# Side work inside a scan tile: its place on VectorE, its distance, PE's sums one tile later, and denser jobs in a four-layer scan network

## The chip, the cores and the metric

The kernel runs on one core of one Trainium2 chip. The metric is device time in microseconds from the first to the last instruction of one execution, with what little lies around it; the number given is the median of the runs. The engines are PE (matrix products), VectorE (DVE), ScalarE (ACT), GpSimd (POOL) and SyncE (SP, which here issues every DMA). Each works through a queue of its own in order.

## The reference

Four images of 64 x 64 positions (L = 4096) with 96 channels go through four layers. Each layer is a mixer and a feed-forward network, both with a residual. Layer 0's mixer is a gated recurrence, those of layers 1 to 3 are selective scans. Cut to what matters, with the convolution, the orders and the feed-forward lines shortened:

```python
def _L0_conv_ref(x, ...):            # gated recurrence, 96 x 16 states
    ...
    def step(h, ins):
        A_t, B_t, C_t, d_t, u_t, g_t = ins
        d = d_t[..., None]
        h_new = d * (A_t * h) + d * (B_t * u_t[..., None])
        y = g_t * jnp.sum(C_t * h_new, axis=-1)
        return (h_new, y)
...
def _L1_conv_ref(x, ...):            # layers 2 and 3 alike
    xz = jnp.einsum('bhwc,ec->bhwe', x, in_proj_w)
    xp, z = jnp.split(xz, 2, axis=-1)
    xc = silu(depthwise_conv_3x3(xp) + conv_b)
    xs2 = jnp.stack([x_hw, x_wh], axis=1)
    xs = jnp.concatenate([xs2, jnp.flip(xs2, axis=-1)], axis=1)
    dts, Bmat, Cmat = jnp.split(x_dbl, [DT_RANK, DT_RANK + D_STATE], axis=2)
    delta = jax.nn.softplus(dts + dt_projs_bias[None, :, :, None])
    ...
    def step(h, inp):
        u_l, dl, b_l, c_l = inp
        dA = jnp.exp(dl[..., None] * A)
        h = dA * h + (dl * u_l)[..., None] * b_l[:, :, None, :]
        y = jnp.einsum('bkdn,bkn->bkd', h, c_l)
        return (h, y)
    ...
    y = _layernorm(y, out_norm_w, out_norm_b)
    y = y * jax.nn.silu(z)
    return jnp.einsum('bhwd,cd->bhwc', y, out_proj_w)
...
h = jax.nn.relu(_qlinear(x, W1, b1))   # feed-forward, products in 8-bit floats
y = _qlinear(h, W2, b2)
```

A selective scan runs over 192 channels with 16 states each, in four orders: by rows, by columns, and both backwards.

## The kernel before

**Stages.** `gated` (line 1039) does layer 0's recurrence for the four images in 384 tiles of 128 x 512. `scans` (line 855) does the selective scans of layers 1 to 3: 12 stages, one for each layer and image, of 384 tiles each. What lies between two recurrences of an image (the sum over orders, the norms, the output product, the feed-forward network, the input product, the 3 x 3 convolution) is a job, `between` (line 612), that is worked off in small steps beside the tiles of another image. Image 3's last job (line 1282) runs alone at the end.

**A scan tile.** A tile is one state n of one chunk of 128 rows (64 channels in each of two orders) over T = 1024 positions. The loop over k (line 986) issues for each tile, in this order: `carry(k-1)` (ScalarE copies the last column of h), `c_rows(k+2)` (SP loads the row of C, spread over the partitions), `decays(k+2)` (ScalarE's exp), `b_rows(k+1)` (PE spreads the row of B into PSUM, the tile bc), `scan(k)` (VectorE's product bc <- du, bc, then its scan h <- da, carry, bc), `times_c(k-1)` (GpSimd multiplies h by C in place), `store` of a finished chunk, the side work, and `accumulate(k-2)` (PE sums h into acc, a double bank in PSUM). There are two bc buffers, so b_rows(k+1) waits for scan k-1; four buffers of h, and one acc.

**Order.** `InOrder` (line 70) chains every instruction of an engine to the one issued before it, so the engines run exactly in the order in which the Python code issues. All instructions are recorded by its inner function, which is why the profile gives line 80 for each of them; they are told apart by the names of their tiles.

**Side work.** It consists of generators. `pump` (line 136) runs a generator up to its next `yield`; `yield True` means that the next piece needs one of two PSUM banks (`bank`, `release`), and a bank comes free at the end of the tile (`settle`). A tile pumps `chain` (prepares the next chunk: dt_proj, softplus; `prepare_chunk`, line 806) and `segment` (the next x_proj with its remainder on VectorE; `prepare_segment`, line 758) once each, and then calls `work`, which lets the job make steps. `Job.step` (line 711) adds `rate` to a credit, capped at 2.0, and pumps every chain of the job's round once per whole credit. A consumer that stands one `yield` behind its producer is therefore one step behind it, which can be in the same tile. A job has rounds: `first` (loads), then `feeds`, `mixers` and `joins` at once, then `second`, then `convolves` and `takes` at once. Norms collect in `pending` until `logarithms` (line 245) takes their Ln together; a strip waits for that. If a stage's job is unfinished 28 tiles before the stage's end, it is worked off there without tiles (lines 999 to 1003).

**The generators that change**: `Norm.measure` (line 227; `moments`, line 209, is VectorE's bn_stats and bn_aggr, tiles st and mv), `join_orders` (line 318; PE's y_t, tile yt), `mixer_out` (line 358; y_c, GpSimd's u times z, out_proj, VectorE's x1), `feed_forward` (line 428; ff_xt, VectorE's xq, ff_h, GpSimd's hq, ff_y, x2), `first` in `between`.

## Time and profile before

| | us |
|---|---|
| median of three runs (20,117.64 to 20,146.91) | 20,146.27 |
| profiled execution | 20,152.58 |
| its span | 20,150.8 |

| engine | busy us | share | instructions |
|---|---|---|---|
| PE | 16,417.6 | 81% | 70,656 |
| VectorE | 17,808.5 | 88% | 13,848 |
| ScalarE | 12,295.0 | 61% | 19,373 |
| GpSimd | 15,531.3 | 77% | 10,470 |

The largest groups are GpSimd's h <- h, c (4608 times 2.358 us), VectorE's scan (4608 times 2.347) and product (4608 times 1.210), and PE's sums into acc (36,864 passes). A busy share over the whole run mixes the gated stage, where VectorE is not the fullest engine, with the scans. PE's clock is granted by a throttle; over the run it is 0.817 of full speed, and a busy PE is not PE at its peak.

### The profile page before, as it was taken

To read this page: it belongs to the slowest core of one execution; us is meant where nothing else is said; L and a number is where in the kernel's file an instruction comes from. 1 tells how busy PE (TensorE), PEld (TensorE's weight loads), DVE (VectorE), ACT (ScalarE), POOL (GpSimd) and SP (SyncE) were. 2 spreads that over 40 slices of the span, in tenths; PEclk is the share of its full clock that TensorE was granted. 3 is DMA by queue.
4 is the path that set the end of the run, shared out by engine and by line. 5 is a ranking of instruction groups with operands and counts; after the bars stand their busy time and mean duration, and the time that the engine had idled before them with its cause. 6 is when DMAs were issued, how large, how long until landed. Compare 5 with 4: busy or idle time off the path is not lost. (4 is left out here: it accounts for less than half of the span.)

```text
span 20150.8 us, 220842 instructions
## 1 busy us (share of the span) xinstructions
PE 16417.6 (81%) x70656; PEld 4838.3 (24%) x70656; DVE 17808.5 (88%) x13848; ACT 12295.0 (61%) x19373; POOL 15531.3 (77%) x10470
## 2 busy tenths in 40 slices
PE   8998788787888787788788888788788888887776
PEld 3332121121122222222222222222222222222223
DVE  6665999999999998999999999989999999999881
ACT  4444665665665665665665666666666666666553
POOL 3434888888888887888888888878888888878882
PEclk9898796786887797897887887887887887888775
DMA  0002666666666666666666676666676666676661
GB/s 20 16 18 69 165 181 174 166 186 167 168 184 171 164 179 175 166 182 180 167 187 171 167 189 167 169 180 169 170 187 171 168 187 168 170 188 161 172 169 44
DMA packets 1234532, 3148.68 MB, mean 156 GB/s; under 512 B 428049, under 2 KB 428177, under 8 KB 1227217
## 3 DMA queue, kind: packets, MB, share of 16 engines
q1 hardware_dynamic: 1233360, 3134.55, 58.6%
q8 instruction: 554, 9.08, 0.2%
q14 instruction: 618, 5.05, 0.1%
HBM read 2819.18 MB, written 314.57 MB: 156 GB/s over the span
## 5 line engine op out<-in xcount | busy, mean ns | idle before, releaser
L80 POOL TENSOR_TENSOR h<-h,c 128x1024 f32<-128x1024 f32 x4608 | 10834.6, 2358 | 2827.5 <-ACT carry L80 1727.5
L80 DVE TENSOR_TENSOR_SCAN h<-da,carry,bc 128x1024 f32<-128x1024 f32 x4608 | 10814.5, 2347 | 608.7 <-POOL carry L80 10.3
L80 PE MATMUL acc<-h,stacked 64*64 64x512 f32 x36864 | 6179.1, 747 | 498.7 <-POOL h L80 493.8
L80 ACT ACTIVATE da<-delta,decay 128x1024 f32<-128x1024 f32 x4608 | 5280.9, 1147 | 1648.9 <-DVE h L80 1601.8
L80 DVE TENSOR_TENSOR bc<-du,bc 128x1024 f32<-128x1024 f32 x4608 | 5574.5, 1210 | 611.2 <-PE bc L80 586.0
L80 PE MATMUL bc<-bs,sel 96*128 96x512 bf16 x9216 | 3346.9, 451 | 2071.8 <-DVE h L80 2054.6
L80 ACT COPY carry<-h 128x1 f32<-128x1 f32 x3456 | 649.0, 188 | 3533.7 <-DVE h L80 3529.1
L80 PEld LDWEIGHTS <-sel 96*128 96x128 bf16 x9216 | 551.3, 101 | 6988.6 <-DVE h L80 5085.7
L80 PEld LDWEIGHTS acc<-h,stacked 64*64 64x64 f32 x36864 | 1132.5, 153 | 3286.5 <-issue 1699.7
L80 ACT ACT_TABLE_LOAD x1133 | 1453.6, 1283 | 41.6 <-DVE mv L80 22.5
L80 POOL TENSOR_TENSOR c<-h,c 128x512 f32<-128x512 f32 x384 | 485.7, 1265 | 970.5 <-ACT c L80 614.8
L80 PE MATMUL conv<-pad,tap_lo 128*128 128x512 f32 x1728 | 917.5, 630 | 0.0
L80 PE MATMUL dt_proj<-rows,w 12*128 12x512 f32 x1152 | 828.0, 805 | 0.0
L80 ACT ACTIVATE du<-e,ones 128x1024 f32<-128x1024 f32 x576 | 660.8, 1147 | 228.8 <-POOL delta L80 223.2
L80 PE MATMUL x_proj_b<-u,xp 128*108 128x512 f32 x1152 | 671.9, 699 | 94.3 <-DMA xp<-in_ssm 59.0
L80 ACT ACTIVATE c<-c,l_bias 128x512 f32<-128x512 f32 x384 | 263.5, 686 | 753.0 <-PE c L80 737.9
L80 POOL TENSOR_TENSOR delta<-delta,du 128x1024 f32<-128x1024 f32 x288 | 679.5, 2359 | 12.1 <-ACT du L80 12.1
L80 POOL TENSOR_TENSOR e<-e,du 128x1024 f32<-128x1024 f32 x288 | 679.4, 2359 | 2.4 <-ACT du L80 2.4
L80 POOL TENSOR_TENSOR du<-delta,u 128x1024 f32<-128x1024 f32 x288 | 679.4, 2359 | 0.7
L80 POOL TENSOR_TENSOR delta<-delta,e 128x1024 f32<-128x1024 f32 x288 | 678.5, 2356 | 0.1
L80 PE MATMUL x_proj_c<-u,xp 128*48 128x512 f32 x1152 | 624.3, 655 | 64.3 <-ACT rows L80 64.3
L80 PE MATMUL conv<-pad,tap_hi 128*128 128x512 f32 (+1 forms) x1152 | 638.5, 650 | 8.2 <-ACT u L80 8.2
(155 smaller groups left out, 16118.3 us busy)
## 6 DMA issues: line engine op xcount, KB each, us to landing
c<-cs SPq DMA_DIRECT2D x9216, 256.0 KB, 4.1
u<-u SPq DMA_DIRECT2D x288, 512.0 KB, 7.6
y<-y SPq DMA_DIRECT2D x1152, 128.0 KB, 2.4
y<-y SPq DMA_DIRECT2D x144, 512.0 KB, 5.6
xr<-x SPq DMA_DIRECT2D x224, 192.0 KB, 4.8
u<-u SPq DMA_DIRECT2D x288, 128.0 KB, 4.4
pad<-y SPq DMA_DIRECT2D x288, 128.0 KB, 4.6
z<-zl SPq DMA_DIRECT2D x96, 256.0 KB, 2.0
```

What stands on the lines that cost most here:

```text
L80: ins = f(*a, **k).ins
```

## The change

Within a tile the side work moves: `scan` takes it as a function, `beside`, and calls it between VectorE's product and its scan. `times_c` and `store` are issued ahead of the product. PE's sums come three tiles behind the scan instead of two, with five buffers of h instead of four. The carries of a new chunk are set to zero at tile 8 of the chunk before. `logarithms` at tile 11 comes behind that tile's carry and decays. The rates go from 1.4 to 1.65 (stage jobs), from 1.9 to 2.6 (the last layer's output jobs) and from 1.4 to 2.6 (layer 0's job), the cap of the credit from 2.0 to 3.0. Several `yield`s are added, and a norm's statistics are taken in three pieces. The halves of chunk 1 are swapped, so that all chunks have the row order first: C then has 32 rows instead of 48, and the selector of B 128 columns instead of 192. GpSimd adds the second bias in one instruction instead of four, and x2 shares xh's buffer.

```diff
-CHUNKS = (((0, 0), (64, 1)), ((0, 1), (64, 0)), ((128, 0), (128, 1)))
+CHUNKS = (((0, 0), (64, 1)), ((64, 0), (0, 1)), ((128, 0), (128, 1)))
...
-NC3 = 48
+NC2 = 2 * NS
...
         def measure(self, src, width, e):
-            mv = moments(src, width)
+            st = sb(5, "st", [128, G, 6])
+            mv = sb(5, "mv", [128, G, 2])
+            for g in range(G):
+                dve.bn_stats(st[:, g, :], src[:, g, 0:width])
+                if g % 2:
+                    yield
+            for g in range(G):
+                dve.bn_aggr(mv[:, g, :], st[:, g, :])
             yield
...
             yield pair == 0
+        yield
         norm = Norm()
...
         normalise(yt, yt, DI, norm.r, norm.nm)
+        yield
         yield True
...
                 pool.tensor_tensor(v[0:m], v[0:m], z[0:m], ALU.mult)
-                yield m == 64
+                yield
+        yield True
         ps = bank("out_proj")
...
             yield
+        yield
         x1 = sb(2, "x1", [128, G, C])
...
         normalise(xh, x1, C, norm.r, norm.nm)
+        yield
         yield True
         ps = bank("ff_xt")
         transpose_strip(ps, xh, 0, C)
+        yield
+        yield
         yield
...
         pool.tensor_copy(hq[:, 2, :], late, saturate=False)
+        yield
         yield True
         ps = bank("ff_y")
...
-        for g in range(G):
-            pool.tensor_tensor(y[:, g, :], y[:, g, :], b[:, 3 : 3 + C], ALU.add)
-        yield
-        x2 = sb(1, "x2", [128, G, C])
+        pool.tensor_tensor(y, y, b[:, None, 3 : 3 + C].to_broadcast([128, G, C]), ALU.add)
+        yield
+        x2 = sb(1, "xh", [128, G, C])
         pool.tensor_tensor(x2, x1, y, ALU.add)
+        yield
         yield
         sp.dma_start(out=tokens(dst, s), in_=x2)
         if layer < 3:
+            yield
             norm = hold["norm", s] = Norm()
...
                 load_y(im, 0, hold)
+            yield
             yield
             yield
...
-            self.credit = min(self.credit + self.rate, 2.0)
+            self.credit = min(self.credit + self.rate, 3.0)
...
+        def start(i):
+            if i.first:
+                carries[i.chunk] = sb(2, f"carry{i.chunk}", [128, NS])
+                pool.memset(carries[i.chunk], 0.0)
+            i.carry = carries[i.chunk]
...
-        def scan(k):
+        def scan(k, beside):
             i, n = tiles[k]
             da, b = live.pop((k, "da")), live.pop((k, "b"))
-            if n == 0 and i.first:
-                carries[i.chunk] = sb(2, f"carry{i.chunk}", [128, NS])
-                pool.memset(carries[i.chunk], 0.0)
-            i.carry = carries[i.chunk]
             dve.tensor_tensor(b, i.du, b, ALU.mult)
-            h = live[k, "h"] = sb(4, "h", [128, T])
+            beside()
+            h = live[k, "h"] = sb(5, "h", [128, T])
...
-                if n == 11:
-                    logarithms()
+                if n == 8 and nxt is not None:
+                    start(nxt)
...
-            if 0 <= k - 1 <= last:
-                carry(k - 1)
-            if k + 2 <= last:
-                c_rows(k + 2)
-                decays(k + 2)
-            if k + 1 <= last:
-                b_rows(k + 1)
-            if k <= last:
-                scan(k)
-            if 0 <= k - 1 <= last:
-                times_c(k - 1)
-            if k >= 3 and (k - 3) % NS == NS - 1:
-                store(items[(k - 3) // NS])
-            if k <= last:
+            def beside():
                 pump(chain)
                 pump(segment)
                 if n == 13:
@@
                     if item.chunk == 2:
                         drain(segment, work)
                 work()
-            if 0 <= k - 2 <= last:
-                accumulate(k - 2)
+
+            if 0 <= k - 1 <= last:
+                carry(k - 1)
+            if k + 2 <= last:
+                c_rows(k + 2)
+                decays(k + 2)
+            if n == 11:
+                logarithms()
+            if k + 1 <= last:
+                b_rows(k + 1)
+            if 0 <= k - 1 <= last:
+                times_c(k - 1)
+            if k >= 4 and (k - 4) % NS == NS - 1:
+                store(items[(k - 4) // NS])
+            if k <= last:
+                scan(k, beside)
+            if 0 <= k - 3 <= last:
+                accumulate(k - 3)
             settle()
...
-        gated(images, Job(between(images[0], 0), patience=1), pl0)
+        gated(images, Job(between(images[0], 0), 2.6, patience=1), pl0)
...
-            jobs[-1].append(Job(between(im, layer - 1), 1.4))
+            jobs[-1].append(Job(between(im, layer - 1), 1.65))
...
-            jobs[-1].append(Job(between(im, 3, im.dst), 1.9))
+            jobs[-1].append(Job(between(im, 3, im.dst), 2.6))
```

## The prediction

> **What bounds the kernel now.** First the page's part 1 and the windows by stage, to split the run; then the waits and the groups of VectorE between 1890 and 19640 us; then the timeline of single tiles. The run is a gated stage (33 to 1750 us), preparations (to 1890), 4608 scan tiles (to 19,679) and a tail (to 20,150.8). Windows (us; PE, PEld, DVE, ACT, POOL busy; clock):
>
> ```profile
> 1640.00:1742.00 102.00, 101.60 (x281) 41.41 (x280) 72.79 (x89) 45.65 (x101) 40.34 (x64) 1.00 0.07 18
> 1742.00:1800.00 58.00, 45.53 (x100) 17.06 (x98) 1.24 (x2) 24.97 (x49) 9.57 (x32) 0.85 0.14 34
> 1800.00:1842.00 42.00, 31.30 (x71) 12.70 (x70) 0.00 (x0) 10.66 (x17) 6.51 (x9) 0.88 0.35 82
> ...
> 1890.00:19640.00 17750.00, 14405.78 (x64735) 3970.86 (x64735) 16511.66 (x11807) 11242.20 (x17195) 14686.67 (x8955) 0.81 0.65 174
> ```
>
> See: PE is full at the end of the gated stage; then 100 us in which VectorE does nothing (the job beside layer 0 is not finished, and runs alone); in the scans VectorE is 93% busy. It is the bound there. One tile of it, then one with side work, from the timeline (start, duration):
>
> ```profile
> 1907.57 1.21 DVE L80 TENSOR_TENSOR bc<-du,bc 128x1024 f32<-128x1024 f32 x1
> 1908.91 2.35 DVE L80 TENSOR_TENSOR_SCAN h<-da,carry,bc 128x1024 f32<-128x1024 f32 x1
> 1911.17 0.71 DVE L80 BATCH_NORM_STATS2 st<-xr 128x6 f32<-128x96 f32 x4
> 1911.80 0.36 DVE L80 BATCH_NORM_AGGREGATE mv<-st 128x2 f32<-128x6 f32 x4
> 1912.08 1.20 DVE L80 TENSOR_TENSOR bc<-du,bc 128x1024 f32<-128x1024 f32 x1
> ```
>
> Product to scan: 1.34 us for a product of 1.21, so 0.13 us idle (the scan reads what the product writes). Scan to next: 2.26 for 2.35, so neighbours that don't depend on each other overlap by 0.09. A plain tile is 3.605 us (mean of the 3739 plain tiles when I list all starts). 4607 x 3.605 = 16,608; first scan to last is 17,787; the excess of 1179 us is 654 of waits and 524 of side work (577 tiles have some). Who VectorE and PE wait for there (us, times, longest):
>
> ```profile
> DVE bc L80 <- PE bc L80: 585.5, 350, 18.0
> DVE xq L80 <- PE ff_xt L80: 24.0, 27, 1.8
> DVE h L80 <- POOL carry L80: 10.3, 7, 1.6
> PE acc L80 <- POOL h L80: 493.1, 374, 5.3
> PE ff_xt L80 <- ACT xh L80: 191.9, 46, 6.1
> ```
>
> Behind each late bc I followed PE's queue back. Largest: out_proj behind GpSimd's u 80 us (34 tiles), ff_xt behind ScalarE's xh 74 (35), PE just busy 63 (63), y_t behind its DMA 59 (11), two layer changes behind xp 36, acc behind GpSimd's h only 44 (44); the rest is spread. An example:
>
> ```profile
> 7963.82 0.74 PE L80 MATMUL out_proj<-w,u 128*128 128x96 f32 x2 [4.51 <-POOL u L80]
> ...
> 7967.09 1.99 PE L80 MATMUL acc<-h,stacked 64*64 64x512 f32 x8
> ...
> 7969.01 0.72 PE L80 MATMUL bc<-bs,sel 96*128 96x512 bf16 x2
> ...
> 7969.77 1.23 DVE L80 TENSOR_TENSOR bc<-du,bc 128x1024 f32<-128x1024 f32 x1 [5.49 <-PE bc L80]
> ```
>
> Side work too close to its producer stops PE's queue, and the scan with it. Last the tail: 471 us after the last scan, with VectorE 21 of 200 us busy. Of image 2's eight last strips one is out before the last scan, the eighth at 19,845.6; image 3's job follows, with its column loads at 19,859.
>
> **The skill.** "VectorE: DVE Perf Modes", The DRAIN you can't avoid, has the next instruction start only when the pipe is empty, and a read after a write on the same engine need a semaphore; its section on two Vector instructions with no wait between them lets one that is not held start earlier. The trace bears out the second and third (0.13 us idle, against 0.09 overlap). "TensorE: Matmul & The Clock Gate", Part 1, says that PE's clock halves after idle windows: acc takes 1.09 or 1.98 us here. The same page calls VectorE's and ScalarE's queues strict FIFO: a waiting side instruction stops the tile's own.
>
> **The change, part by part** (against the profiled execution: 20,152.6 us, span 20,150.8; the median, 20,146.3, lies 6 us lower).
>
> 1. *Side work between product and scan.* Today a run of side instructions of length D costs D - 0.09 (the x_proj remainder: 0.66, measured excess 0.60). Between product and scan it overlaps at both ends and covers the 0.13 us: D - 0.30, a gain of 0.21 per tile. If a product does not let its successor overlap (the trace never shows that pair; product after product in the gated stage has a gap of 0.03), it is D - 0.19, a gain of 0.10. A norm's statistics are split over three steps, so more tiles get side work: counting yields under the kernel's rules (credit, two banks, logarithms) gives 576 tiles before (the trace has 577) and 883 after. D in all: 524 + 577 x 0.09 = 573, plus 26 of image 2's strips (part 4), plus some 25 for lost overlaps at the cuts: 624. New cost 624 - 883 x 0.30 = 360, gain 164; with 0.19, 456, gain 68. I take 140.
>
> 2. *Distance, rate 1.65, sums three tiles behind.* At 1.4 steps a tile, a consumer one step later falls into the same tile in 0.4/1.4 = 29% of cases. Two steps at 1.65 are never the same tile. out_proj and ff_xt get the second step: 154 us to some 30. ff_y likewise (18 to 8), y_t's first load a step of 2.2 us (59 to 40). Sums: PE's 493 us behind GpSimd go, but only 44 of them reached VectorE; to 5. Together -200. Against it: unchanged one-step pairs fall together more often (0.65/1.65 = 39%); convolutions get denser (a strip every 15.4 tiles for 18.3 by the count; a strip is some 17 us of PE at full clock: 30 convolution passes and 8 of in_proj and z at 0.43, which is what back-to-back passes take in the timeline, and the transposes; so +0.17 us per tile on a PE that is 88% busy there, 105.9 of 120 us at 14,497): +50. VectorE's side work now stands before the scan, 2.3 us earlier against ScalarE and PE; the added yields cover st, x1 and xq, but the remainder (190 times, one tile behind ScalarE) is uncovered: 0 to 40, taken 10. Last stage at 2.6: two steps can be one tile again (23%), and 24 strips for 17: waits 109 to some 150, +40. Sum -100. Bounds: -250 (all the gain, no cost) and +150 (convolutions at PE's limit, clock low).
>
> 3. *Carries ahead, logarithms after the decays, job finished earlier.* The 10 us behind carry go. At two layer changes the job's rest was worked off without scans just ahead of the next loads (SP busy 4.9 us with part_c); by the count the job ends 11 tiles ahead now: -20 of 36 + flush. GpSimd's four bias adds in one, fewer selector copies, 32 for 48 C rows: beside GpSimd's 17% idle, nothing. SP: x2's store is issued a step later, so blocks the c loads behind it less; nothing. Sum -30.
>
> 4. *Last stage at 2.6.* The same count for 1.9 puts image 2's first out strip at tile 369 (the trace: 370), the others after the scans. For 2.6 with the new yields all eight lie before tile 373 of 384, so the tail is image 3 alone. From the last scan: about 16 us to sums, store and landing, then as today from the column loads: 20,151 - 19,859 = 292. 308 for 471: -163. I take -160. If two strips slip out of the scans it is -120.
>
> 5. *Layer 0's job at 2.6.* The count finishes it at gated tile 330 of 384 (1.4: three of eight convolved, the trace agrees). The 92 us from 1750 to 1842 go. But PE's 77 us of it (45.5 + 31.3 above) move into a stage where PE is 99% busy once convolutions run; earlier windows leave some idle. Cost 60 to 84, taken 67: -25 (0 to -60).
>
> Sum: -140 - 100 - 30 - 160 - 25 = -455: 20,152.6 - 455 = 19,698, near 19,695 on the median's side.
>
> **Rivals.** (a) As summed: 19,695, own range 19,560 to 19,830; chance 0.52. (b) Distance only changes who waits: VectorE's side work waits itself for ScalarE and PE, and the product doesn't overlap. For: in-order queues, and the step rate rises with the yields. Against: two steps are a full tile. Leaves 160 + 25 + 30: 19,935; 0.23. (c) PE is never late except for its DMAs: waits 654 to 250, parts 1 and 5 at their best (164, 40), tail 160: -768, 19,380. For: PE never waits for GpSimd. Against: dense convolutions; 0.17. (d) Slower: PE becomes the bound in the dense stretches. At the low clock a tile's bc and acc are 1.04 + 1.98 us, with the shares of x_proj and dt_proj (0.4 at full clock) and of a convolution strip (17/15.4 = 1.1), doubled, 6 us; 11 x 108 convolution tiles and 384 of the last stage are 1570. From 0.3 us per such tile on (PE's mean over about 4 us) it eats 455; at 0.4 us: 20,320. Against: the clock is 0.87 to 0.94 in those windows, as PE is busy; 0.08.
>
> Chances: (a), (c) and most of (b) and a little of (d): faster 0.91, within 0.2% (about what this measurement can tell from no change) 0.03, slower 0.06. The range goes to (c) below and (b) above: 19,470 to 19,920.
>
> **What would show it.** Side work standing between product and scan with no idle ahead of the scan, tile excess D - 0.30. "PE acc behind POOL h" near zero; "DVE bc behind PE bc" near 400. No VectorE hole after the gated stage, last gated scan later by some 65 us. All of image 2's stores before the last scan, tail near 310. Wrong, if VectorE waits for ScalarE or PE in st, x, xq or rows by more than 100 us, or if PE's clock in the convolution windows falls.

## The result and the profile after

The changed kernel takes 20,024.88 us (median of five runs, 20,018.46 to 20,055.13); the kernel before, run on the same chip, takes 20,135.62. The ratio is 0.9949, 95% interval 0.9935 to 0.9964: faster by 0.5%, where 2.2% was forecast, and outside the forecast's range. The profiled execution has a span of 20,016.7 us, 134.1 less than that of before (the medians differ by 111: the profiled execution is the fastest of the five after, and the one before, at 20,152.58, lies above all five of before). (In the changed kernel the recording line is L78, for L80, and PE's sums read `twice` where they read `stacked`.)

The page, its first part and the groups of the scan:

```profile
PE 16405.8 (82%) x70656; PEld 4828.9 (24%) x70656; DVE 17721.0 (89%) x13832; ACT 12306.6 (61%) x19398; POOL 15475.3 (77%) x10086
...
L78 DVE TENSOR_TENSOR_SCAN h<-da,carry,bc 128x1024 f32<-128x1024 f32 x4608 | 10797.4, 2343 | 507.3 <-ACT norm L78 23.0
...
L78 PE MATMUL acc<-h,twice 64*64 64x512 f32 x36864 | 6198.0, 749 | 11.3 <-POOL h L78 10.8
...
L78 DVE TENSOR_TENSOR bc<-du,bc 128x1024 f32<-128x1024 f32 x4608 | 5571.2, 1209 | 656.2 <-PE bc L78 630.3
```

VectorE's instructions take what they took (the scan 2.343 us for 2.347, the product 1.209 for 1.210); the difference lies in its idle time and in where things stand. Splitting both traces in the same way, by the listing of all starts, gives the whole difference in four numbers (us):

| | before | after | difference |
|---|---|---|---|
| first scan tile starts (gated stage and preparation) | 1890.3 | 1958.9 | +68.6 |
| first to last scan: side work on VectorE | 524 | 338 | -186 |
| first to last scan: waits of VectorE | 654 | 817 | +163 |
| last scan to the end | 471.0 | 291.4 | -179.6 |

The middle two are what the 4607 steps from scan to scan take beyond 3.605 us each; 17,786.8 became 17,763.7 in all. Of the 186 us of side work, 159 stand in the tiles that have some and 27 in those that have none, which came out a little shorter (3.599 us for 3.605). So two parts of the change bring 366 us, and two others take 232 of them back.

Side work in its new place, read from the timeline of the changed kernel (the last column is the idle time of the engine before the instruction, and what ended it):

| start us | us | engine | instruction | waited before |
|---|---|---|---|---|
| 19629.05 | 1.21 | DVE | TENSOR_TENSOR bc<-du,bc x1 |  |
| 19630.17 | 0.54 | DVE | TENSOR_TENSOR x<-xr,out_proj x1 |  |
| 19630.74 | 0.74 | DVE | BATCH_NORM_STATS2 st<-x x4 |  |
| 19631.40 | 2.33 | DVE | TENSOR_TENSOR_SCAN h<-da,carry,bc x1 |  |
| 19633.65 | 1.21 | DVE | TENSOR_TENSOR bc<-du,bc x1 |  |
| 19634.76 | 0.37 | DVE | BATCH_NORM_AGGREGATE mv<-st x4 |  |
| 19635.05 | 2.32 | DVE | TENSOR_TENSOR_SCAN h<-da,carry,bc x1 |  |

The x starts 1.12 us after the product, which lasts 1.21: the product does let its successor overlap. The aggregate of 0.37 us makes its step 3.65 us, from 19631.40 to 19635.05, only some 0.05 more than a step without side work.

The groups above end in the idle time ahead of each group, and in who ended most of it: 630.3 us of the product's 656.2 lie behind PE's bc. The view of the waits, between 1958 and 19,680 us, has the other pairs (a selection of its rows):

| engine, tile | waits for | us | times | longest |
|---|---|---|---|---|
| DVE bc | PE bc | 630.3 | 335 | 21.3 |
| DVE rows | ACT bs | 42.2 | 21 | 4.0 |
| DVE st | DMA xr<-x | 30.9 | 16 | 3.1 |
| DVE x | PE out_proj | 25.2 | 21 | 3.4 |
| DVE st | ACT yt | 15.6 | 15 | 2.0 |
| PE acc | ACT y | 169.2 | 151 | 3.3 |
| PE in_xt | ACT xh | 132.8 | 41 | 8.6 |
| PE y_c | ACT yt | 80.1 | 29 | 5.0 |
| PE out_proj | POOL u | 79.3 | 40 | 5.4 |
| PE ff_xt | ACT xh | 47.8 | 36 | 4.1 |
| ACT xh | POOL norm | 348.4 | 136 | 7.2 |

PE's 493 us behind GpSimd's h are gone (7.9 are left), and ff_xt's 191.9 are 47.8. But VectorE's lateness behind PE, which was to fall to some 400, rose to 630, and a second kind stands beside it: VectorE itself waits in side work, 148 us in all for 41 before. Behind each late bc I followed PE's queue back again: out_proj 49 us (80 before), ff_xt 2 (74), acc 17 (44), y_t 78 (59); but in_xt behind ScalarE's xh 128 (3 before), y_c behind ScalarE's yt 65 (3), and PE just busy 124 (63). One in_xt, in the timeline:

| start us | us | engine | instruction | waited before |
|---|---|---|---|---|
| 7129.36 | 1.54 | ACT | ACTIVATE xh<-xr,norm x4 | 4.99 for POOL norm |
| 7129.88 | 1.52 | PE | MATMUL in_xt<-ident,xh x4 | 8.64 for ACT xh |
| 7131.33 | 1.99 | PE | MATMUL acc<-h,twice x8 |  |
| 7133.25 | 1.03 | PE | MATMUL bc<-bs,sel x2 |  |
| 7134.32 | 1.23 | DVE | TENSOR_TENSOR bc<-du,bc x1 | 6.54 for PE bc |

Read it upwards: VectorE is 6.54 us late for its row of B; the row stood in PE's queue behind the sums and those behind in_xt, which had waited 8.64 us for ScalarE, and ScalarE 4.99 us for GpSimd's norm. This is the pattern that the forecast showed for out_proj, one generator further on.

The stretches ahead of the scans, from the windows by stage:

| window us | length | PE busy | DVE busy | ACT busy | POOL busy | PE clock |
|---|---|---|---|---|---|---|
| 1477 to 1700 | 223 | 221.10 | 139.91 | 110.94 | 84.60 | 1.00 |
| 1700 to 1906 | 206 | 188.83 | 149.28 | 74.88 | 76.03 | 0.93 |
| 1906 to 1958 | 52 | 23.18 | 4.92 | 21.25 | 16.56 | 0.72 |

The hole of 100 us is gone, as forecast: the preparation takes 52 us, for 152. But the last gated scan comes at 1906.6 instead of 1738.0. The four images take 431.5, 482.6, 515.1 and 429.2 us, for 402.8, 438.6, 423.5 and 424.7. The first image has no job beside it at all, and is 29 us longer.

Last, the tail. All of image 2's stores are out before the last scan: the latest (out <- xh) is issued at 19,683.56, the last scan starts at 19,722.55. The page's row of VectorE's busy tenths in 40 slices, of some 500 us each, ends in a 4: in 291 of the last slice's 500 us the job of image 3 stands alone. In the kernel before the row ended in a 1, with 471 us of a slice of 504:

```profile
DVE  6656999999999999999999999999999999988884
```

### The profile page after: what moved, and what is told of

Same layout as the page of the kernel before. It is cut to its first block, busy times and chain, and to the rows that moved or that the text cites. A ratio compares the mean times of both kernels' runs of the same rounds, so it can differ in the third digit from the quotient of the medians.

```text
span 20016.7 us, 220305 instructions
## 1 busy us (share of the span) xinstructions
PE 16405.8 (82%) x70656; PEld 4828.9 (24%) x70656; DVE 17721.0 (89%) x13832; ACT 12306.6 (61%) x19398; POOL 15475.3 (77%) x10086
## 5 line engine op out<-in xcount | busy, mean ns | idle before, releaser
L78 POOL TENSOR_TENSOR h<-h,c 128x1024 f32<-128x1024 f32 x4608 | 10832.7, 2359 | 2723.7 <-ACT carry L78 1730.5
L78 DVE TENSOR_TENSOR_SCAN h<-da,carry,bc 128x1024 f32<-128x1024 f32 x4608 | 10797.4, 2343 | 507.3 <-ACT norm L78 23.0
L78 ACT ACTIVATE da<-delta,decay 128x1024 f32<-128x1024 f32 x4608 | 5280.9, 1148 | 1507.9 <-DVE h L78 1492.8
L78 PE MATMUL acc<-h,twice 64*64 64x512 f32 x36864 | 6198.0, 749 | 11.3 <-POOL h L78 10.8
L78 DVE TENSOR_TENSOR bc<-du,bc 128x1024 f32<-128x1024 f32 x4608 | 5571.2, 1209 | 656.2 <-PE bc L78 630.3
L78 PE MATMUL bc<-bs,sel 96*128 96x512 bf16 x9216 | 3388.1, 456 | 2351.0 <-DVE h L78 2338.8
L78 ACT COPY carry<-h 128x1 f32<-128x1 f32 x3456 | 648.7, 188 | 3203.7 <-DVE h L78 3198.8
L78 PEld LDWEIGHTS <-sel 96*128 96x128 bf16 x9216 | 551.1, 101 | 7287.9 <-DVE h L78 5440.5
L78 PEld LDWEIGHTS acc<-h,twice 64*64 64x64 f32 x36864 | 1130.6, 153 | 2798.4 <-issue 1924.1
L78 POOL TENSOR_TENSOR c<-h,c 128x512 f32<-128x512 f32 x384 | 485.5, 1264 | 1149.4 <-ACT c L78 783.5
L78 PE MATMUL conv<-pad,tap_lo 128*128 128x512 f32 x1728 | 927.1, 647 | 0.0
L78 ACT ACTIVATE du<-e,ones 128x1024 f32<-128x1024 f32 x576 | 661.2, 1148 | 352.3 <-POOL delta L78 347.5
L78 PE MATMUL dt_proj<-rows,w 12*128 12x512 f32 x1152 | 823.5, 801 | 6.8 <-ACT delta L78 6.8
L78 PE MATMUL x_proj_b<-u,xp 128*108 128x512 f32 x1152 | 707.5, 732 | 47.5 <-DMA xp<-in_ssm 12.6
L78 ACT ACTIVATE c<-c,l_bias 128x512 f32<-128x512 f32 x384 | 263.1, 685 | 772.6 <-PE c L78 771.2
L78 PE MATMUL x_proj_c<-u,xp 128*32 128x512 f32 x1152 | 625.0, 656 | 79.7 <-ACT rows L78 71.2
L78 POOL TENSOR_TENSOR delta<-delta,du 128x1024 f32<-128x1024 f32 x288 | 679.4, 2359 | 7.8 <-ACT du L78 7.8
L78 POOL TENSOR_TENSOR e<-e,du 128x1024 f32<-128x1024 f32 x288 | 679.3, 2359 | 2.4 <-ACT du L78 2.4
L78 POOL TENSOR_TENSOR du<-delta,u 128x1024 f32<-128x1024 f32 x288 | 680.3, 2362 | 0.1
L78 POOL TENSOR_TENSOR delta<-delta,e 128x1024 f32<-128x1024 f32 x288 | 678.5, 2356 | 0.1
L78 PE MATMUL conv<-pad,tap_hi 128*128 128x512 f32 (+1 forms) x1152 | 597.4, 620 | 3.5 <-ACT u L78 3.5
```

The source lines that it names most:

```text
L78: ins = f(*a, **k).ins
```

## The experiments

Fourteen more kernels ran. "First scan", "side", "waits" and "tail" are as in the table above, from the profiled execution; "late product" is a VectorE bc behind PE's bc. Single profiled executions are not all typical: e7's is the slowest of its four, 29 us above their median, and e10's is the fastest of its four, 42 us below it. Where a profile and the medians tell different things, both are given.

| kernel | median us | ratio to before (95%) | first scan | side | waits | tail |
|---|---|---|---|---|---|---|
| before | 20,135.62 | | 1890.3 | 524 | 654 | 471.0 |
| after | 20,024.88 | 0.9949 (0.9935 to 0.9964) | 1958.9 | 338 | 817 | 291.4 |
| e3_behind | 20,106.80 | 0.9987 (0.9980 to 0.9993) | 1959.2 | 526 | 726 | 291.7 |
| e9_before_place | 20,340.05 | 1.0104 (1.0089 to 1.0119) | 1883.2 | 384 | 971 | 473.6 |
| e5_sums_two | 20,124.09 | 0.9995 (0.9986 to 1.0003) | 1958.0 | 343 | 925 | 292.3 |
| e1_whole_l0 | 19,950.74 | 0.9914 (0.9899 to 0.9929) | 1864.5 | 338 | 848 | 291.5 |
| e2_l0_job_14 | 20,087.51 | 0.9978 (0.9969 to 0.9987) | 2007.5 | 338 | 852 | 291.6 |
| e6_out_19 | 20,043.36 | 0.9962 (0.9948 to 0.9976) | 1960.9 | 327 | 793 | 349.5 |
| e8_before_out26 | 20,157.92 | 1.0015 (1.0008 to 1.0022) | 1889.3 | 539 | 821 | 291.6 |
| e7_in_xt | 19,903.46 | 0.9887 (0.9872 to 0.9902) | 1920.3 | 337 | 771 | 291.7 |
| e10_both | 19,881.33 | 0.9872 (0.9858 to 0.9887) | 1864.9 | 333 | 737 | 291.5 |
| e12_own | 19,829.13 | 0.9850 (0.9835 to 0.9864) | 1860.8 | 357 | 714 | 291.6 |
| e11_slow_conv | 19,788.03 | 0.9837 (0.9820 to 0.9853) | 1868.0 | 336 | 660 | 291.7 |
| e13_y_c | 20,033.75 | 0.9957 (0.9943 to 0.9971) | 1866.5 | 337 | 900 | 317.3 |
| e14_y_c_165 | 19,902.08 | 0.9883 (0.9866 to 0.9899) | 1869.3 | 346 | 781 | 294.9 |
| e15_y_c_16 | 19,914.08 | 0.9892 (0.9877 to 0.9907) | 1892.5 | 340 | 772 | 294.3 |

**The place alone.** Two kernels: the changed one with its side work put back behind the scan, and the kernel before with nothing changed but the place (side work between product and scan, times_c and store ahead of it).

```diff
             dve.tensor_tensor(b, i.du, b, ALU.mult)
-            beside()
             h = live[k, "h"] = sb(5, "h", [128, T])
...
                 op1=ALU.add,
             )
+            beside()
```

> The changed kernel with the side work issued behind the scan again instead of between product and scan; yields, rates, sums and all else as changed. Theory G (the place gains 0.21 us per tile with side work, and costs VectorE waits of its own): the side cost beyond waits rises from 338 to about 530 us (883 tiles by 0.21), VectorE's own waits in st, x, xq and rows fall from 148 to under 50; in all 80 to 110 slower than the changed kernel, 20,105 to 20,135. Theory W (the place is what made the waits grow by 164 us): the waits fall from 818 to 650 or less, and the time is the same or lower, 20,000 to 20,040.

> The kernel before with the side work between product and scan, and nothing else of the change but times_c and store issued ahead of the product. Theory G (the place gains 0.21 us for each of 577 tiles and costs VectorE waits where its side work stands too close behind ScalarE and PE; the added yields are what keeps these down): side cost from 524 to about 400, VectorE's own waits from 41 to 150 or more; 20,110 to 20,200. Theory W' (the place alone carries the gain, the yields only lengthen the jobs): own waits under 80, 20,030 to 20,060.

The place pays in side work what was forecast or more: 526 to 338 in the changed kernel, 524 to 384 in the old one. It does not keep it. VectorE's own waits are 18 us in e3 for 148 in the changed kernel, and the median differs by 82, not by 188. In the old kernel the edit costs 1%, 140 us more than the slowest that was expected of it. There VectorE waits in its scan for the carries, as the page's groups show (compare the changed kernel's scan above: 23.0 is the most that one releaser has there):

```profile
L80 DVE TENSOR_TENSOR_SCAN h<-da,carry,bc 128x1024 f32<-128x1024 f32 x4608 | 10802.5, 2344 | 644.0 <-POOL carry L80 130.0
...
L80 DVE TENSOR_TENSOR bc<-du,bc 128x1024 f32<-128x1024 f32 x4608 | 5569.3, 1209 | 498.5 <-PE bc L80 471.3
```

and in the view of the waits:

| engine, tile | waits for | us | times | longest |
|---|---|---|---|---|
| DVE xq | PE ff_xt | 153.3 | 78 | 4.2 |
| DVE st | POOL x | 70.8 | 45 | 4.0 |

and in e3:

| engine, tile | waits for | us | times | longest |
|---|---|---|---|---|
| DVE bc | PE bc | 667.1 | 351 | 21.8 |
| DVE rows | ACT bs | 8.0 | 7 | 2.1 |
| DVE st | DMA xr<-x | 4.2 | 5 | 1.0 |

What waited 24 us for ff_xt behind the scan waits 153 ahead of it; VectorE's own waits in side work are 351 us in all, for 41. Side work ahead of the scan is issued a scan's length (2.3 us) earlier against its producers, and its wait holds the scan up at once. The zeroed carries, 130 for 10, have another cause: in this edit `times_c(k-1)` is issued ahead of the product, and the memset of a new chunk's carries, still issued in `scan`, now queues on GpSimd behind the product with C of the tile whose scan has only just ended. In the kernel before it stood ahead of that product (for 72 memsets the scan now waits 71 times, for 7). So this edit as a whole is a loss in the old kernel, and 120 us of its waits belong to `times_c` and not to the side work. In the changed kernel, which has the added steps and the early carries, the place pays; what each of the two contributes was not run apart.

**The sums.** PE's sums two tiles behind the scan again, with the five buffers kept.

```diff
-        for k in range(last + 5):
+        for k in range(last + 4):
...
-            if k >= 4 and (k - 4) % NS == NS - 1:
-                store(items[(k - 4) // NS])
+            if k >= 3 and (k - 3) % NS == NS - 1:
+                store(items[(k - 3) // NS])
...
-            if 0 <= k - 3 <= last:
-                accumulate(k - 3)
+            if 0 <= k - 2 <= last:
+                accumulate(k - 2)
```

> The changed kernel with PE's sums two tiles behind the scan again (five buffers of h stay). If the third tile matters to VectorE (theory T): PE's waits for GpSimd's product ahead of the sums come back to some 490 us, the late products behind PE grow by 50 or more, 20,075 or slower. If PE had that time to spare (theory N: only 44 us of late products stood behind those waits before the change): PE waits 490 us again and the time moves by less than 40, 19,985 to 20,065.

It costs 99 us, all of the change's gain. PE's wait for GpSimd's h comes back (498.3 us in the whole run, for 10.8 in the changed kernel and 493.1 in the scans of the kernel before), and VectorE's behind PE grows from 630.3 to 769.2:

```profile
L78 PE MATMUL acc<-h,twice 64*64 64x512 f32 x36864 | 6260.8, 756 | 504.2 <-POOL h L78 498.3
L78 DVE TENSOR_TENSOR bc<-du,bc 128x1024 f32<-128x1024 f32 x4608 | 5571.8, 1209 | 795.8 <-PE bc L78 769.2
```

Late products behind it are 104 us in 80 tiles, where the kernel before had 44 in 44. Taking the cost of a wait from what reached VectorE in the kernel before made it too small by more than half. Why is not settled. That the same wait reaches VectorE more often beside the job's denser steps is one reading. Another is that PE's queue was not followed back far enough: taken back to PE's last wait for a free bc buffer, the same trace of before has 79 us in 77 tiles behind GpSimd's h, and e5 has 175 in 129. The third tile alone, in the kernel before, was not run.

**Layer 0.** The split statistics stand also in the gated stage, in the preparation of each strip. e1 takes them whole there; e2 puts the job's rate back.

```diff
-        def measure(self, src, width, e):
+        def measure(self, src, width, e, whole=False):
...
-                if g % 2:
+                if g % 2 and not whole:
                     yield
...
-            yield from norm.measure(st.xr, C, 1e-6)
+            yield from norm.measure(st.xr, C, 1e-6, True)
```

> The changed kernel, but the statistics of the norm that prepares a strip of layer 0 are taken in one step again (no yields between the pieces there). Theory S (the two extra yields shift each strip's preparation, so that its transposes l_xt and the products behind them meet the closing of the strip before): image 0 of the gated stage, which has no job beside it, falls from 431 us to about 403, all four images lose about 28 us each, the first scan tile comes near 1850 instead of 1959, in all about 19,910. Theory P (the stage grew by 169 us because the denser job's PE work moved into it): image 0 stays at 431, at most 10 us are gained, 20,015.

```diff
-        gated(images, Job(between(images[0], 0), 2.6, patience=1), pl0)
+        gated(images, Job(between(images[0], 0), 1.4, patience=1), pl0)
```

> The changed kernel with layer 0's job at 1.4 steps a tile instead of 2.6 (the statistics stay split). Theory S: image 0 stays at 431 us, images 1 and 2 fall from 483 and 515 to about 460, but the rest of the job runs alone after the last gated tile for more than 100 us, so that the first scan tile comes no earlier than 1959 (to 2010): 20,025 to 20,075. Theory P: with the old rate the stage is as before, first scan tile near 1890, 19,955.

With whole statistics the first image takes 403.0 us again, the first scan starts at 1864.5, and the median falls by 74. That is 40 less than was expected: the fourth image got no faster (436.8 us for 429.2). Against the kernel before the first scan is 26 us earlier: the gated stage is 75 us longer (1738.0 to 1812.6) and what follows it 100 shorter, the two terms of the forecast. The rate itself is right, too: at 1.4 (under the new cap) the first scan comes 49 us later, as expected, and the median, 20,087.51, lies 13 above its expected range. What the two steps did is to move a strip's preparation by two tiles, against the closing of the strip before it. From the timeline of the changed kernel, first image:

| start us | us | engine | instruction | waited before |
|---|---|---|---|---|
| 163.70 | 1.03 | PE | MATMUL l_out<-e,h x8 |  |
| 166.74 | 1.54 | ACT | ACTIVATE bs<-x,norm x4 | 2.54 for POOL norm |
| 167.26 | 1.52 | PE | MATMUL l_xt<-ident,bs x4 | 2.53 for ACT bs |
| 168.57 | 3.62 | PE | MATMUL bc<-rows,u x4 |  |
| 172.23 | 0.75 | DVE | SCALAR_TENSOR_TENSOR da<-bc,l_bias,y x1 | 5.71 for PE bc |

and of the kernel before:

| start us | us | engine | instruction | waited before |
|---|---|---|---|---|
| 158.04 | 1.39 | PE | MATMUL l_xt<-ident,bs x4 | 2.15 for ACT bs |
| 162.60 | 0.75 | DVE | SCALAR_TENSOR_TENSOR da<-bc,l_bias,delta x1 | 3.03 for PE bc |
| 163.54 | 1.03 | PE | MATMUL l_out<-e,h x8 |  |

There l_xt had its own tile ahead of l_out, and VectorE was 3.03 us late; now l_xt follows l_out in the next one, and it is 5.71.

**The last stage.** The changed kernel with the old rate of 1.9 in its last stage, and the kernel before with the new rate and cap alone.

```diff
-            jobs[-1].append(Job(between(im, 3, im.dst), 2.6))
+            jobs[-1].append(Job(between(im, 3, im.dst), 1.9))
```

> The changed kernel with the output jobs of the last layer at 1.9 steps instead of 2.6. Theory L (the tail is set by how many strips of image 2 are left): four strips are left after the last scan, the tail grows from 291 to about 380 us, the waits of the last stage fall from 164 to about 110; in all 20,060. Theory K (the strips cost the same wherever they stand): within 20 us of 20,025.

```diff
-            jobs[-1].append(Job(between(im, 3, im.dst), 1.9))
+            jobs[-1].append(Job(between(im, 3, im.dst), 2.6))
...
-            self.credit = min(self.credit + self.rate, 2.0)
+            self.credit = min(self.credit + self.rate, 3.0)
```

> The kernel before with one part of the change alone: output jobs at 2.6 steps, credit cap 3.0; no added yields. By the count of yields all strips of image 2 are out at tile 291 of 384. Theory L: the tail falls from 471 to about 291 us, the last stage's waits grow from 109 to 200 or less (one-step pairs now share a tile in 62% of cases instead of 47%); in all 19,990 to 20,060 against 20,135. Theory K: within 20 us of 20,135.

The tail follows the rate: 349.5 at 1.9, where some 380 was expected, 291.4 at 2.6, and 291.6 in the kernel before with 2.6. (Under the old cap of 2.0 a rate of 1.9 makes one step and two in turn, 1.5 a tile; e6, with the new cap, really has 1.9.) But it is bought in the scans. Neither median is what the theory of the tail expected: e6's lies within 20 us of the changed kernel's, as its rival said, and e8's, 20,157.92 for an expected 19,990 to 20,060, is even slower than before. e8 gains 179 us of tail and loses 181 in the scans: 96 in the last stage, 85 in the eleven others, where the higher cap lets stage jobs make more steps, too. In the changed kernel 2.6 for 1.9 brings 58 us of tail for 34 of waits in the last stage; the medians differ by 18, and their intervals overlap.

**Close pairs.** One step more between ScalarE's xh and PE's in_xt (e7); this with e1 (e10); and on top of e10 one more step before each of three pieces of VectorE's side work that wait, the x_proj remainder, x1 and the statistics of a loaded strip (e12).

```diff
         normalise(xh, xr, C, norm.r, norm.nm)
+        yield
         yield True
         ps = bank("in_xt")
```

> The changed kernel with one more yield between the normalised strip (ScalarE's xh) and the transposes in_xt of the next layer's input, the one pair of this kind that the change left one step apart. Theory D (a pair one step apart falls into one tile more often at 1.65 steps than at 1.4, and then stops PE's queue): the 128 us of late products behind in_xt fall under 30, 90 us faster, 19,930. Theory R (PE is late because convolutions stand denser; which pair PE waits in is chance): the waits show up behind another pair, within 25 us of 20,025.

> The changed kernel with both mended: layer 0's preparation takes its statistics in one step, and in_xt stands one yield further behind xh. If the two are independent, the gains add: first scan tile near 1850 or earlier, waits of the scans near 770, in all 19,950 - 121 = 19,830. If they share their gain in the gated stage (the wait behind in_xt took 39 us there too, in image 2): 19,860 to 19,880.

> Both mended, and one more yield each ahead of VectorE's remainder (rows, behind ScalarE's bs), its x1 (behind PE's out_proj) and its first statistics in layer 0's job (behind the load xr). If VectorE's own waits are a matter of distance: from 146 to under 80 us, 50 to 70 faster than without these. If what is saved comes back as late products (longer strips, other pairs meeting): within 20 us.

e7 gains 121 us in the median, 39 of them in the third gated image. That leaves some 82 for the scans; the two profiled executions, e7's slowest and the changed kernel's fastest, show 48. PE's wait of in_xt for xh is 35.2 us, for 132.8, and VectorE's late products behind it fell from 128 us to 24; the waits in the scans as a whole fell by 46. The same step on top of e1 tells more. e10's first scan comes at 1864.9, for 1864.5, so the step brings nothing in the gated stage beside e1, and the gains of e1 and e7 don't add up there (e10 came within 2 us of what was expected if they share that gain). In the scans the waits fell by 111 us (848 to 737), about as much as the late products, whose groups follow, first in e1, then in e10:

```profile
L78 DVE TENSOR_TENSOR bc<-du,bc 128x1024 f32<-128x1024 f32 x4608 | 5570.5, 1209 | 677.3 <-PE bc L78 650.8
```

```profile
L78 DVE TENSOR_TENSOR bc<-du,bc 128x1024 f32<-128x1024 f32 x4608 | 5568.6, 1208 | 580.0 <-PE bc L78 546.7
```

The median fell by 69; e10's profiled execution is its fastest. So of the 104 us of late products that the step took away, the medians show 69 to 82 in the scans; the profiles scatter from 46 to 111.

e12 is less clear. VectorE's own waits went from 141 us to 74, late products from 547 to 607, side work from 333 to 357, and the scans took 17,678.5 us for 17,678.7 in the two profiles. But e10's is its fastest and e12's is not, and e12's median is 52 below e10's, with intervals of the ratios that overlap (e10 from 0.9858, e12 up to 0.9864). Whether e12 beats e10 stays open.

**Density of the convolutions.** e10 with the stage jobs at 1.5 in their last round, which convolves.

```diff
-            self.chains, self.done = [], False
+            self.chains, self.done, self.round = [], False, 0
...
-            self.credit = min(self.credit + self.rate, 3.0)
+            rate = 1.5 if self.round == 4 and self.rate == 1.65 else self.rate
+            self.credit = min(self.credit + rate, 3.0)
...
                     self.chains = next(self.rounds, None)
+                    self.round += 1
```

> The same, and the round of convolutions of the stage jobs at 1.5 steps a tile instead of 1.65 (all still finished before tile 352 by the count). Theory R (the denser convolutions make PE late: some 140 us of late products had PE simply busy, 63 before the change): the waits in the second part of the stages fall by 50 us or more, 40 faster than without. Theory D (only pairs that stand too close cost): no change beyond 20 us.

e11 is the fastest kernel of the study: 93 us below e10, 237 below the changed kernel. VectorE's product waits in e11 (e10's line stands above):

```profile
L78 DVE TENSOR_TENSOR bc<-du,bc 128x1024 f32<-128x1024 f32 x4608 | 5568.2, 1208 | 544.4 <-PE bc L78 518.8
```

The waits in the convolution part of the stages (from the tile of the first in_xt on) fell from 283 to 200 (358 in the changed kernel, 237 before). In stages 4 to 10, but for stage 7, the convolutions ran from tile 205 to 345 in the kernel before, 20 tiles for each of seven strips; from 216 to 333 in the changed one, 16.7; from 219 to 348 in e11, 18.4. That the lower rate pays is shown; that it pays because PE has more room is not. Late products make up only 28 of the 83 us (210 to 182), and those for which PE was just busy did not fall (81 to 107 in this part, with PE's queue followed back to the end of the scan that frees the buffer). Some 50 us are VectorE's waits for ScalarE: its remainder behind bs went from 30 to 12 us, its scan behind the copied carries from 17 to under 1, and behind the decays from 16 to 2. A lower rate also lets fewer one-step pairs share a tile (0.5/1.5 = 33% for 39%), and the two were not run apart.

**Too far.** e11 with one more step between ScalarE's yt and PE's y_c, the next pair in the list; and the same at 1.65 and at 1.6 in the convolutions.

```diff
         normalise(yt, yt, DI, norm.r, norm.nm)
         yield
+        yield
         yield True
         g = []
```

> e11_slow_conv with one more yield between ScalarE's normalised yt and PE's y_c. In e11 VectorE's late products behind y_c, waiting for yt, are 51 us in 21 tiles; PE's own waits of y_c for yt are 85 us. Theory G (a pair of ScalarE and PE that can fall into one tile costs what it shows, and a step takes it away, as with in_xt): these 51 us fall to about 10, the scans lose 30 to 50 us, and the median is about 19,750. Rival H (saved waits come back as other late products, as those of VectorE's own waits did): the 51 us fall as well, but the waits in all stay within 15 us of 660, and the median stays within 15 us of 19,788.

> e10_both with the extra yield between yt and y_c; the convolutions are at 1.65 again. In e13 the last convolution fell on tile 357 of a stage, where the job is worked off without tiles from tile 356 on (348 in e11). Theory D (e13 lost its time to this limit): the last convolution here is at about 343, the waits of the stages' last 64 tiles are as in e10, the 18 us waits at the changes of layer are gone, and the time is at or below e10's 19,881: 19,840 to 19,890. Rival P (the extra step itself shifts the rest of the job against the tiles, and the distance that helped in_xt hurts here): about 20,050, near e13.

> e13_y_c with the convolutions at 1.6 instead of 1.5. Theory D: the last convolution comes at about tile 349, ahead of the limit at 356; e13's 240 us come back but for the denser convolutions: 19,780 to 19,850. Rival P: near e13, 20,000 or more.

Both theories fell with e13: it lost 246 us. The late products behind y_c did go (51 us to none behind yt), but the first convolution moved from tile 219 to 228, and the last from 348 to 356, the tile from which the job is worked off without tiles. At a change of layer, in the timeline of e13:

| start us | us | engine | instruction | waited before |
|---|---|---|---|---|
| 7541.44 | 1.03 | PE | MATMUL bc<-bs,sel x2 | |
| 7547.80 | 2.35 | DVE | TENSOR_TENSOR_SCAN h<-da,carry,bc x1 | |
| 7563.27 | 3.72 | PE | MATMUL x_proj_b<-u,xp x4 | 20.80 for DMA xp<-in_ssm |
| 7568.30 | 0.61 | PE | MATMUL bc<-bs,sel x2 | |
| 7568.94 | 1.23 | DVE | TENSOR_TENSOR bc<-du,bc x1 | 18.79 for PE bc |

The next layer's first rows are stored so late that their load is awaited with nothing left to scan. The loads of u come late as well: the page's group of these products waits more than three times as long as in the changed kernel, first its line there, then in e13:

```profile
L78 PE MATMUL x_proj_b<-u,xp 128*108 128x512 f32 x1152 | 707.5, 732 | 47.5 <-DMA xp<-in_ssm 12.6
```

```profile
L78 PE MATMUL x_proj_b<-u,xp 128*108 128x512 f32 x1152 | 685.3, 711 | 169.8 <-DMA u<-u 80.4
```

In the last 32 tiles of stages 3 to 10 the waits are 197 us, for 47 in e11: 150 of the 240 that all waits rose by. e14 ends at tile 342 or 343 in these stages and takes back 132 us, e15 ends at 344, but at the limit in stages 3 and 7, where 48 us of waits are left in the last 32 tiles, and takes back 120. So the limit is shown as the cause of the larger part. Both came out above what the theory of the limit expected, e14 by 12 us and e15 by 64; the rest of e13's loss was not traced. And e14 against e10, with no limit in either, says what the step itself is worth: 21 us slower in the median with intervals that overlap, waits 781 for 737 (e10's profile is its fastest). Here the waits that were taken away came back elsewhere, so far as can be told.

## Why the forecast was right and wrong

By its own steps, against the profiled execution; steps 2 and 3 both act on the waits, and are measured together:

| step | forecast | measured |
|---|---|---|
| 1, the place | -140 | -186 |
| 2 and 3, distance, rate, sums; carries | -100 and -30 | +163 |
| 4, the last stage | -160 | -180 |
| 5, layer 0's job | -25 | +69 |
| sum | -455 | -134 |

**Step 1 was right** in its mechanism: a product lets its successor overlap. The value taken lay between its bounds on the low side; the tiles with side work gave 159 us, near the 164 of the better bound (excess per run of side work: the remainder 0.53 to 0.37, where the forecast had read 0.60; xq 0.59 to 0.37; x1 0.45 to 0.26). The number of tiles with side work, 883 by the count, is 884. (573 in the forecast's sum should be 576, which changes nothing.) That tiles without side work became shorter as well, 27 us, was not foreseen.

**Step 2 failed.** The forecast wrote "Together -200" of the pairs that the change pulls apart, and put "+50", "0 to 40, taken 10" and "+40" against it, -100 in all; its sign was a bc behind PE "near 400", and it is 630. Of what was pulled apart, out_proj and ff_xt behaved roughly as sized, 154 to 51 us (30 forecast); y_t's 59 did not fall but rose to 78. The pairs that stayed one step apart were given no price of their own, and VectorE's side work was given too small a one:

- "unchanged one-step pairs fall together more often (... 39%)" had no price but that of the convolutions. in_xt and y_c, 6 us before, are 193 after. Two things were missed. The cap: at 1.4 with a cap of 2.0 the jobs had in fact made four steps in three tiles, 1.33, so 1.65 is 24% denser and not 18%, and one-step pairs shared a tile in 25% of cases before, not in 29%. And the chain of two: GpSimd's norm, ScalarE's xh and PE's in_xt are one step apart each. By the count under the kernel's rules norm and xh now fall into one tile 33 times in 88 for 13, and PE's wait for xh contains ScalarE's for the norm (262 us before, 348 after). e7 and e10 show that in_xt costs: 121 us and 69 in the medians. For y_c no run shows it: e14 put one step more there and gained nothing.
- VectorE's remainder and its other side work: 41 to 148 us, for the 10 taken. e3, with 18, and e9, with 351, show that it belongs to the place. The forecast's sign of being wrong, over 100 us behind ScalarE or PE, was just missed (95); the rest is behind the loads and GpSimd.
- The convolutions themselves were about as sized. The waits in that part of the stages rose by 121 (237 to 358), for the 50 taken, but in_xt lies in it: with that pair one step further apart and the strips as dense, e10 has 283 there, 47 above before. The strips stand 16.7 tiles apart for 20, 20% denser; the count of the forecast, 15.4 for 18.3, had 19%. e11, at 18.4, gains 83 us of these waits.
- The sums, 39 us in the forecast (44 to 5), are worth 99 in the changed kernel: a term in the other direction, without which the change gains nothing (e5).

The waits in the part with feeds, mixers and joins fell a little, from 308 to 296; they rose in the convolution part and in the last stage (109 to 164).

**Step 3** did what it says. The waits for carry are gone, and those in the last 32 tiles of stages 3 and 7 fell from 42.5 us to 2.5.

**Step 4 was right**, tail and cost: 55 us of waits in the last stage for the 40 taken. e8 adds that without the rest of the change the cost eats the gain whole (85 of its 181 us lie in the other stages, where its cap works too).

**Step 5** was sized rightly and is not the whole of it: e1 has the -26. The other 95 us, from 1864.5 to 1958.9, come from two steps inside `Norm.measure`, which the forecast counted only for the scans. It did not ask who else runs that generator.

Of the rivals, (b) came nearest, and its first half came true in part: VectorE's side work waits itself, and some saved waits came back elsewhere; but e10 shows that distance at in_xt does pay, and the product does overlap, against its second half. Its price of 19,935 was too low because it left step 2 at nothing and step 5 at its gain, by more than the gain of step 1 that it left out; that price lay just outside the forecast's own range, which ended at 19,920. Of (d), PE too full in the dense stretches, at most a third came true: 121 us over 11 x 108 convolution tiles is 0.10 us per tile, where it was to decide from 0.3, and most of that is in_xt. PE's clock did not fall there: over the tiles with convolutions it is 0.92 before and after (in the scans as a whole 0.814 before, 0.808 after).

## What to carry to other kernels

In a hand-ordered pipeline the waits of one pair are not simply a saving. A step more before in_xt took away some 104 us of late products and brought 69 to 82 in the scans by the medians; the step before y_c (e14) took away a wait of the same kind and brought nothing, and e12's gain is not clear of the noise. So price a pair by putting it apart and measuring, and give a price to the pairs that you leave as they are when the rate goes up. An added step also lengthens the job: look how far the job's end is from its limit (e13 lost 246 us, the larger part of it there). One rate need not fit all rounds of a job; lowering it in one of them gave the fastest kernel here (e11). And before an edit to a shared helper, list all its callers, and price what the edit shifts in each stage.

## What was not expected of the hardware

- The same instructions in the same order took different times in different kernels. The scans of the changed kernel, e1 and e2 are the same code and took 17,763.7, 17,794.2 and 17,797.4 us; in e14 and e15, whose gated stages are the same code, the second image took 442.2 and 457.4. Executions of one kernel differ as well: e11's four lie between 19,768 and 19,838 us. So a difference of some 30 us between single profiled executions is no effect by itself.
- PE's 493 us of waits for GpSimd seemed covered, with 44 reaching VectorE. They were worth 99 us in the changed kernel (e5). That other waits on PE shared the same cover would explain it, but no run here shows it.
